# A block's weighted row sum in four column groups, and a bias product in two row groups and two banks: one change to a two-layer attention and expert kernel

## The chip, the cores and the metric

The kernel runs on one core of a Trainium2 chip. The time is device microseconds (us) of one execution; of the kernel before, three runs were timed, and a further one was profiled. The engines are TensorE (PE in the profile; its weight loads are PEld), VectorE (DVE), ScalarE (ACT), GpSimd (POOL) and SyncE (SP, which issues most DMAs).

## What is computed

Four sequences of 512 rows of 256 numbers go through two layers; each layer is an attention with a context of 1024 rows, and a mixture of experts of which each row takes two.

```python
# layer 0's attention (encoder_hc: the normed x; decoder_hq: the context)
Sim = (encoder_hc @ w1)[:, :, None] + (decoder_hq @ w2)[:, None, :] + jnp.einsum('bid,bjd->bij', encoder_hc * w3, decoder_hq) + b_sim[0]
A = jax.nn.softmax(Sim, axis=2)
hq_hat = jnp.einsum('bij,bjd->bid', A, decoder_hq)
Batt = jax.nn.softmax(jnp.max(Sim, axis=2), axis=1)
hc_bar = jnp.einsum('bi,bid->bd', Batt, encoder_hc)[:, None, :]        # the weighted row sum
feats = jnp.concatenate([encoder_hc, hq_hat, encoder_hc * hq_hat, encoder_hc * hc_hat], axis=-1)
hcq = feats @ W_qv + b_qv
...
# layer 1's experts: comb is a row's weight for each of 8 experts (two are not zero)
for e in range(8):
    a = jax.nn.gelu(_layernorm(xf, ln_w[e], ln_b[e]) @ fc1_w[e] + fc1_b[e], approximate=True)
    out = out + (a @ fc2_w[e] + fc2_b[e]) * comb[:, e:e + 1]           # fc2_b: the experts' biases
```

Two places of this are changed: `hc_bar`, the sum of a block's 512 rows with one weight each, and the sum over experts of `fc2_b[e] * comb[:, e]`, which the kernel makes for all rows by itself, as a product of `comb` and `fc2_b`.

## The kernel before

All data are 32-bit floats. A batch is 512 rows, four tiles of 128. The program is written with a tile framework whose scheduler orders each engine's instructions; TensorE's order is as written for the whole program, SP's for the experts' stages.

**Stages.** Layer 0's attention (`layer0_attention`, about 10 to 215 us) goes through the four batches: scores against the context (L315), softmax, transposes of the probabilities (L274), the attended context (L345), and the products with `W_qv` (L381). Work of neighbouring batches is interleaved by hand: `sim_finish` is a generator that is advanced piece by piece, between another batch's scores and transposes, and the routing of the batch before is a third strand. Then come layer 0's experts (to about 365), layer 1's attention (`layer1_attention`, to about 640) and layer 1's experts (the rest).

**The row sum** (`sim_finish`). With `mx` the rows' maxima, `gb` minus the block's maximum (one number copied to 128 partitions by L354), ACT makes `eb = exp(mx + gb)`, 128 partitions by four tiles, and its sum `es` (L359). L364 sums `es` over the partitions, L366 multiplies each tile's column of `eb` with the tile's 128x256 rows and accumulates the four in one row of PSUM, L370 and L372 divide on VectorE, and L393 turns the row of 256 into two columns of 128, which scale a part of `W_qv` (`weff`, L399). The order on TensorE about it: scores of the next batch (L315; in the last batch the routing's product L888), L364, L366, products L381.

**Layer 1's attention** runs 32 units (batch, tile, pair of heads). TensorE's order in one step: scores of a unit (L616, two groups of 64 array rows), first half of an older unit's transposes (a2t, L639, two banks of four), the output product of an older one (L679), its values (L664, two groups of 64 array columns) and a transpose (L670), a piece of the routing and the bias product, a piece of the next queries, and the second half of the a2t transposes. VectorE makes the scores' minimum with the mask (L625), ACT the exponential (L629), both copy the transposes from PSUM (L642, L644).

**The bias product** (`route_steps` with layer 1). `comb` (L980) is 128 x 4 tiles x 8 experts. L984 transposes the four tiles into 8 partitions x 512, L986 copies that on ACT, and L994 multiplies: for each pair of tiles two products of 8x128 with `fc2b` (8x256) into the two halves of one bank; L998 adds a pair to `x` on VectorE. The pairs of a batch are one step apart, except in the last batch. After the last one come the stores of `x` (L1000) and, for the last batch, the remaining scatters of rows (L951), two behind each entry of `L.biased`; layer 1's experts read those rows.

**PSUM.** Three pools of two buffers each: `ps_s` for scores, `ps_t` (`tr_ps`, transposes and small things) and `ps_m` (`mm_ps`, products). A tile of a pool waits for the release of the one before the last of that pool.

**Other lines that matter.** Gates' logits L888 use four groups of 32 array columns:

```python
nc.tensor.matmul(
    lt_ps[t * GROUP : t * GROUP + GROUP, :], gates[:, c, :], xT[:, c, bass.ts(t, P)],
    start=(c == 0), stop=(c == NC - 1),
)
```

GpSimd clears constants at the start, then issues the fills of the row buffers (L200, L207), which wait for the last first load, and adds `bqv` to `x` (L295). `wsim_row` (L305, for the last time at 173.5 us) and `bqv` (L295, 132.8 us) are single constants of 128x256.

Of the kernel before, what the change touches and what calls it, by code (L numbers as in the profile page):

```python
# [8 lines left out]
F32 = mybir.dt.float32  # L9
# [3 lines left out]
AF = mybir.ActivationFunctionType  # L13
ALU = mybir.AluOpType
# [3 lines left out]
P = 128  # L18
NB = 4
S = 512  # L20
NT = S // P
M = 1024
NJ = M // P
D = 256
# [3 lines left out]
EX = 8  # L28
# [8 lines left out]
GROUP = 32  # L37
# [26 lines left out]
def two_layers(ctx: ExitStack, tc: tile.TileContext, io, out):  # L64
    nc = tc.nc

    const = ctx.enter_context(tc.tile_pool(name="const", bufs=1))
# [4 lines left out]
    sm = ctx.enter_context(tc.tile_pool(name="sm", bufs=4))  # L72
# [9 lines left out]
    def t4(shape, name, dt=F32):  # L82
        return k4.tile(shape, dt, tag="k4", name=name)
# [4 lines left out]
    def tsmall(shape, tag, dt=F32):  # L88
        return sm.tile(shape, dt, tag=tag, name=tag, bufs=2 if tag[:3] in ("rt_", "tp_", "tt_") else None)
# [4 lines left out]
    def tr_ps(name):  # L94
        return ps_t.tile([P, 512], F32, tag="t", name=name)

    def mm_ps(name):
        return ps_m.tile([P, 512], F32, tag="m", name=name)


    ident = const.tile([P, P], F32, tag="ident", name="ident")
    make_identity(nc, ident)
    ones = const.tile([P, P], F32, tag="ones", name="ones")
# [40 lines left out]
    def small(name, shape, src, queue=nc.sync):  # L144
        t = const.tile(shape, F32, tag=name, name=name)
        queue.dma_start(out=t, in_=src)
        return t
# [5 lines left out]
    x = []  # L153
# [21 lines left out]
    bqv = small("bqv", [P, D], io["b_qv"].partition_broadcast(P), nc.gpsimd)  # L175
    wsim_row = small("wsim_row", [P, D], io["w_sim_row"].partition_broadcast(P), nc.gpsimd)
# [13 lines left out]
        nc.sync.dma_start(out=gates[:, :, at : at + n], in_=src.rearrange("(c p) e -> p c e", p=P))  # L190
    gate_b = small("gate_b", [P, ET0], io["expert_bias"].partition_broadcast(P))
    alpha = small("alpha", [P, EX], io["alpha"].partition_broadcast(P))
    fc2b = small("fc2b", [EX, D], io["fc2_b"])
    wq = small("wq", [P, NC, D], io["Wq"].rearrange("(c p) n -> p c n", p=P))
    wkv = small("wkv", [P, NC, 2 * D], io["Wkv"].rearrange("(c p) n -> p c n", p=P))
    wo = small("wo", [P, NC, D], io["Wo"].rearrange("(c p) n -> p c n", p=P))
# [2 lines left out]
    for e in range(EX):  # L199
        i = nc.gpsimd.dma_start(  # L200
            out=rows[e * REGION : (e + 1) * REGION, :].rearrange("(p k) r -> p k r", p=P),
            in_=zeros.unsqueeze(1).to_broadcast([P, REGION // P, ROW]),
# [5 lines left out]
        out=ys[:, :].rearrange("(p k) d -> p k d", p=P),  # L208
        in_=zeros[:, 0:D].unsqueeze(1).to_broadcast([P, 2 * NB * S // P, D]),
# [100 lines left out]
    def sim_scores(st, t):  # L310
# [12 lines left out]
        softmax_exp(p, spf, 1.0, nm)  # L323
        return p

    def sim_finish(st):

        b, xn, eT, aT = st["b"], st["xn"], st["eT"], st["aT"]

        mx = tsmall([P, NT], "b0_mx")  # L330
        nc.vector.scalar_tensor_tensor(mx, st["r"], bsim, st["negmax"], ALU.add, ALU.subtract)
        m1 = tsmall([P, 1], "b0_m1")
        nc.vector.tensor_reduce(m1, mx, AX.X, ALU.max)
        gp = tr_ps(f"g0_{b}")
        nc.tensor.transpose(gp[0:1, 0:P], m1, ident)
        g = tsmall([1, 1], "b0_g")
        nc.vector.tensor_reduce(g, gp[0:1, 0:P], AX.X, ALU.max, negate=True)

        hq = t4([P, NC, S], f"hqT_{b}")
        eh = t4([P, NC, S], f"ehT_{b}")  # L340

        def attend(c):
            op = mm_ps(f"hq_{b}_{c}")
            for j in range(NJ):
                nc.tensor.matmul(  # L345
                    op, ctxn[b][:, j, bass.ts(c, P)], aT[:, j, :], start=(j == 0), stop=(j == NJ - 1)
                )
            nc.scalar.copy(hq[:, c, :], op)
            st["attended"] = nc.vector.tensor_tensor(eh[:, c, :], op, eT[:, c, :], ALU.mult)

        attend(0)
        yield
        bp = tr_ps(f"gb0_{b}")
        nc.tensor.matmul(bp[:, 0:1], ones[0:1, :], g, start=True, stop=True)  # L354
        gb = tsmall([P, 1], "b0_gb")
        nc.vector.tensor_copy(gb, bp[:, 0:1])
        eb = tsmall([P, NT], "b0_eb")
        es = tsmall([P, 1], "b0_es")
        nc.scalar.activation(eb, mx, AF.Exp, bias=gb, accum_out=es)  # L359
        attend(1)  # L360
        yield

        hp = tr_ps(f"hc0_{b}")
        nc.tensor.matmul(hp[0:1, D : D + 1], es, ones[:, 0:1], start=True, stop=True)  # L364
        for t in range(NT):
            nc.tensor.matmul(  # L366
                hp[0:1, 0:D], eb[:, t : t + 1], xn[:, t, :], start=(t == 0), stop=(t == NT - 1)
            )
        rt = tsmall([1, 1], "b0_rt")
        nc.vector.reciprocal(rt, hp[0:1, D : D + 1])  # L370
        hr = sm.tile([1, D], F32, tag="b0_hr", name=f"b0_hr_{b}", bufs=1)
        nc.vector.tensor_scalar(hr, hp[0:1, 0:D], rt, None, ALU.mult)  # L372
        ops = {}

        def products(t, k, last):
            if not last:
                ops[t] = mm_ps(f"hcq_{b}_{t}")[:, 0:D]
            op = ops[t]
            for c in range(NC):
                for i, (l, w) in enumerate(k):  # L380
                    nc.tensor.matmul(  # L381
                        op, l[:, c, bass.ts(t, P)], w(c), start=(not last and c == 0 and i == 0),
                        stop=(last and c == NC - 1),
                    )

        late = [(hq, lambda c: wqv[:, 2 + c, :]), (eh, lambda c: wqv[:, 4 + c, :])]
        for t in range(2):
            products(t, late, False)
        yield

        hp = tr_ps(f"hcc0_{b}")
        for c in range(NC):
            nc.tensor.matmul(hp[:, c : c + 1], hr[:, bass.ts(c, P)], ones[0:1, 0:1], start=True, stop=True)  # L393
        hc = tsmall([P, NC], "b0_hc")
        nc.vector.tensor_copy(hc, hp[:, 0:NC])

        weff = sm.tile([P, NC, D], F32, tag="weff", name=f"weff_{b}", bufs=1)
        for c in range(NC):
            nc.vector.scalar_tensor_tensor(  # L399
                weff[:, c, :], wqv[:, 6 + c, :], hc[:, c : c + 1], wqv[:, c, :], ALU.mult, ALU.add  # L400
            )
        yield
        for t in range(NT):
            if t >= 2:
                products(t, late, False)
            products(t, [(eT, lambda c: weff[:, c, :])], True)
            nc.vector.tensor_tensor(x[b][:, t, :], ops[t], x[b][:, t, :], ALU.add)
            if t > 0:
                yield
# [122 lines left out]
    def mha_bias(st, t):  # L532

        if t == 0:
            st["mbias"] = t8([P, NT, M], f"mbias_{st['b']}", BF16)
        return nc.vector.tensor_scalar(
            st["mbias"][:, t, :], st["mask"][:, t, :], 1.0, MASKED, ALU.subtract, ALU.mult
        )
# [143 lines left out]
    def layer1_attention(sts):  # L682
# [3 lines left out]
        units = []  # L686
        for b in range(NB):
            units += [(b, t, n) for t in range(NT) for n in range(NC)]
        ps, aTs = {}, {}
        routes, queries = {}, None  # L690
        kvs = mha_kvs(sts, (NB - 1,))
        done = None
        for i in range(len(units) + 4):
            if i < len(units):
                b, t, n = units[i]
                ps[i] = mha_scores(sts[b], n, t)
                unit = sts[b]
                if i + 1 < len(units) and units[i + 1][0] > 0 and units[i + 1][2] == 0:
                    bias = mha_bias(sts[units[i + 1][0]], units[i + 1][1])
# [4 lines left out]
            if 0 <= i - 2 < len(units):  # L704
                b, t, n = units[i - 2]
# [5 lines left out]
            if 0 <= i - 4 < len(units):  # L711
                b, t, n = units[i - 4]
                if n == NC - 1:
                    added = mha_out(sts[b], t)
            if 0 <= i - 3 < len(units):
                b, t, n = units[i - 3]
# [11 lines left out]
            b = i // (2 * NT) + 1  # L728
# [9 lines left out]
            b, k = divmod(i - 11, 2 * NT)  # L738
# [76 lines left out]
    L1 = Layer(1, EX, FF1 // P, ET0, None)  # L815
# [57 lines left out]
    def route_steps(L, b):  # L873
# [12 lines left out]
        for c in range(NC):  # L886
            for t in range(NT):
# [3 lines that stand above are left out]
# [13 lines left out]
        buf, xn = st["buf"], st["xn"]  # L904
        shape = [P, 2, NT, ne]
        pick = tsmall(shape, "rt_pick")
# [17 lines left out]
        at = tsmall([P, NT, ne], "rt_atp")  # L924
# [45 lines left out]
        if L.n == 0:  # L970
            for t in range(NT):
                xs = x[b][:, t, :]
# [3 lines left out]
            return  # L976

        nc.vector.tensor_tensor(pick, pick, wk.unsqueeze(3).to_broadcast(shape), ALU.mult)
        comb = tsmall([P, NT, EX], "rt_comb")
        nc.vector.tensor_tensor(comb, pick[:, 0], pick[:, 1], ALU.add)  # L980
        yield
        cp = tr_ps(f"cT_{b}")
        for k in range(NT):
            nc.tensor.transpose(cp[0:EX, bass.ts(k, P)], comb[:, k, :], ident)  # L984
        cT = t4([EX, S], f"combT_{b}")
        nc.scalar.copy(cT, cp[0:EX, :])  # L986
        yield
        L.biased = []
        for k in range(0, NT, 2):
            if k > 0 and b + 1 < NB:  # L990
                yield
            op = mm_ps(f"b2_{b}_{k}")
            for j in range(2):
                nc.tensor.matmul(  # L994
                    op[:, bass.ts(j, D)], cT[:, bass.ts(k + j, P)], fc2b, start=True, stop=True
                )
            xs = x[b][:, k : k + 2, :]
            L.biased.append(nc.vector.tensor_tensor(xs, op.rearrange("p (j d) -> p j d", d=D), xs, ALU.add))  # L998
        written.append(
            nc.sync.dma_start(out=flat[b * S : (b + 1) * S, :].rearrange("(t p) d -> p t d", p=P), in_=x[b])  # L1000
        )
# [476 lines left out]
```

## Time and profile before

| what | us |
|---|---|
| timed runs | 918.59 (median), 915.99, 918.94 |
| the profiled execution | 917.38 |
| its span, first to last instruction | 915.60 |
| PE busy, 47 to 200 us (153.0) | 148.7 |
| PE busy, 400 to 520 us (120.0) | 117.0 |
| PE busy, 520 to 600 us (80.0) | 75.8 |
| VectorE busy, 520 to 600 us | 57.0 |
| ScalarE busy, 520 to 600 us | 49.8 |
| PE busy, 640 to 690 us (50.0) | 46.5 |
| PE busy, 690 to 916 us (225.6) | 215.8 |

How to read the lines below. A group's line has: line, engine and operation, what it writes <- what it reads, shapes (for a matmul, array rows * columns in use, then the shape), count | busy us, mean ns of one | idle before it, and what ended the idle time. A timeline's line has start, length in us, engine, line, operation, count, and in brackets the idle time before it with its releaser. Neighbouring records of one group are merged, and a matmul's length reaches to its modelled end, so that of two lines of PE the starts say more than the lengths. A product of 32-bit floats is two matmul records, a transpose one. All times are of the one profiled execution, counted from its first instruction.

### The profile page before, as it was taken

Reading aid. Unit: us, or ns where it says so; the run is one execution under the profiler, and the core shown is the slowest. Engines: PE = TensorE matmul, PEld = TensorE weight load, DVE = VectorE, ACT = ScalarE, POOL = GpSimd, SP = SyncE. Lnnn points to the kernel's source line nnn. Section 1 sums busy time; section 2 is a strip of 40 time slices with the busy share of each in tenths; the row PEclk is TensorE's granted clock in tenths of the full one; section 3 lists DMA queues with packets and bytes.
Section 4 is the critical chain, followed back from the end, with each engine's and each line's share of the span. In section 5 each row is a group of like instructions: output and inputs, shape, how many; then the busy total and the mean of one; then the engine's idle time right before and its main releaser. Section 6 shows DMA issues by size and latency. Waiting matters only on the chain.

```text
span 915.6 us, 15375 instructions
## 1 busy us (share of the span) xinstructions
PE 868.2 (95%) x5578; PEld 659.9 (72%) x5578; DVE 426.1 (47%) x1253; ACT 334.2 (36%) x749; POOL 226.2 (25%) x276
## 2 busy tenths in 40 slices
PE   6899999998999998999999999999989999999995
PEld 2456464755699996556676666667879999999995
DVE  5646473736623331765675686676721111111120
ACT  4323331222211111475574565565512333222231
POOL 2303014044313222000130250351642122122122
PEclk9999999999999999999999999999999999999999
DMA  8999933030188893600000123221257956877961
GB/s 309 293 261 245 246 134 112 15 101 35 54 276 262 252 347 116 229 24 1 24 2 1 46 69 119 71 70 56 74 158 247 304 168 193 262 238 239 322 213 22
DMA packets 55028, 142.08 MB, mean 155 GB/s; under 512 B 6894, under 2 KB 32933, under 8 KB 48800
## 3 DMA queue, kind: packets, MB, share of 16 engines
q1 hardware_dynamic: 39264, 102.89, 33.5%
q0 software_dynamic: 15392, 38.10, 16.4%
q8 instruction: 48, 0.79, 0.3%
q14 instruction: 36, 0.29, 0.1%
q10 hardware_dynamic: 288, 0.00, 0.0%
HBM read 131.52 MB, written 39.91 MB: 187 GB/s over the span
## 4 chain that ended last, share of the span: by engine, by line
PE 43%; DVE 7%; issue 4%; ACT 4%; DMA 2%; POOL 0%; SPq 0%; POOLq 0%; ACTq 0%; DVEq 0%
PE hp L1145 12%; PE y L1170 11%; PE s L616 5%; PE a2t L639 4%; PE o L664 4%; ACT p L629 2%; DVE p L625 2%; PE q L600 1%; ACT a2T L644 1%; PE hp_ahead L1145 1%; PE ht L1120 1%; PE wo L679 1%; DMA ys<-yw,to 1%; PE o L670 1%; DMA yb<-ys 1%
## 5 line engine op out<-in xcount | busy, mean ns | idle before, releaser
L1154 ACT ACTIVATE aT<-hp,w1s 128x128 f32<-128x128 f32 x248 | 67.3, 382 | 163.3 <-issue 153.2
L1145 PEld LDWEIGHTS hp<-hT,w1s 128*128 128x128 f32 x992 | 115.8, 192 | 2.4 <-DVE hT L1126 0.8
L1145 PE MATMUL hp<-hT,w1s 128*128 128x128 f32 x992 | 116.1, 275 | 0.6 <-DVE hT L1126 0.6
L1170 PE MATMUL y<-w2s,aT 128*128 128x256 f32 x496 | 112.3, 379 | 0.5 <-ACT aT L1154 0.5
L1170 PEld LDWEIGHTS y<-w2s,aT 128*128 128x128 f32 x496 | 91.8, 190 | 11.9 <-ACT aT L1154 0.7
L629 ACT ACTIVATE p<-p,s_nm 128x1024 f32<-128x1024 f32 x64 | 73.5, 1148 | 73.3 <-DVE s_nm L625 73.2
L625 DVE CUSTOM_DVE_ANT_0 p<-s,mbias 128x1024 f32<-128x1024 f32 x64 | 75.7, 1221 | 38.7 <-PE s L616 38.6
L1188 POOL DMA_INDIRECT out<-yw,to x31 | 47.8, 1541 | 168.1 <-DMA out<-yw,to 59.6
L1174 DVE TENSOR_SCALAR yw<-y,row 128x256 f32<-128x256 f32 x59 | 28.6, 484 | 122.3 <-PE y L1170 122.3
L951 POOL DMA_INDIRECT rows<-rowbuf,rt_posi x64 | 64.2, 1004 | 81.8 <-DVE rt_posi L931 25.4
L639 PEld LDWEIGHTS a2t<-ident,p 128*128 128x128 f32 x512 | 56.2, 142 | 36.8 <-issue 21.7
L639 PE MATMUL a2t<-ident,p 128*128 128x128 f32 x512 | 70.8, 278 | 5.7 <-DVE xn2T L594 2.6
L616 PE MATMUL s<-kT,q2T 64*128 64x512 f32 x256 | 65.1, 615 | 0.7 <-DVE s_nm L625 0.7
L664 PE MATMUL o<-a2T,v 128*64 128x128 f32 x1024 | 63.3, 276 | 0.1
L315 PE MATMUL s<-ctxT,q0T 128*128 128x512 f32 x128 | 62.4, 634 | 0.7 <-ACT q0T L292 0.7
L664 PEld LDWEIGHTS o<-a2T,v 128*64 128x64 f32 x1024 | 55.4, 137 | 8.5 <-issue 6.8
L644 ACT COPY a2T<-a2t 128x512 f32<-128x512 f32 x96 | 53.3, 582 | 16.1 <-PE a2t L639 16.1
L1126 DVE TENSOR_SCALAR hT<-ht,w1s 128x128 f32<-128x128 f32 x62 | 22.6, 406 | 77.3 <-PE ht L1120 71.2
L345 PE MATMUL hq<-a0T,ctxn 128*128 128x512 f32 x128 | 56.8, 596 | 0.1
L1145 PEld LDWEIGHTS hp<-hT,w0s 128*128 128x128 f32 x448 | 54.3, 192 | 3.2 <-DVE hT L1122 1.8
L1145 PE MATMUL hp<-hT,w0s 128*128 128x128 f32 x448 | 55.0, 276 | 1.0 <-DVE hT L1122 1.0
L1170 PE MATMUL y<-w0s,aT 128*128 128x256 f32 x224 | 53.1, 380 | 0.7 <-ACT aT L1150 0.7
(258 smaller groups left out, 1206.8 us busy)
## 6 DMA issues: line engine op xcount, KB each, us to landing
w1s<-in_w1p SPq DMA_DIRECT2D x34, 1030.0 KB
w2s<-in_w2p SPq DMA_DIRECT2D x34, 1024.0 KB
rows<-zeros POOLq DMA_DIRECT2D x8, 2064.0 KB
w0s<-in_w1p SPq DMA_DIRECT2D x31, 512.0 KB
w0s<-in_w2p SPq DMA_DIRECT2D x31, 512.0 KB
row<-rows SPq DMA_DIRECT2D x59, 129.0 KB
ctxT<-in_ctxT SPq DMA_DIRECT2D x4, 1024.0 KB
ctxn<-in_ctx SPq DMA_DIRECT2D x4, 1024.0 KB
```

Source lines behind the costliest of these rows:

```text
L315: nc.tensor.matmul(sp[:, h, :], st["qT"][:, c, bass.ts(t, P)], ctxT[b][:, c, bass.ts(h, 512)], start=(c == 0), stop=(c == NC - 1),)
L345: nc.tensor.matmul(op, ctxn[b][:, j, bass.ts(c, P)], aT[:, j, :], start=(j == 0), stop=(j == NJ - 1))
L616: nc.tensor.matmul(sps[r][:, k, :], st["qT"][at, n, bass.ts(t, P)], st["kT"][at, n, bass.ts(k, 512)], start=True, stop=True,)
L625: nc.vector.tensor_tensor_reduce(p, sps[r].rearrange("p h n -> p (h n)"), st["mbias"][:, t, :], -ATT_SCALE, -ATT_SCALE * LEAST, ALU.add, A ...
L629: nc.scalar.activation(p, p, AF.Exp, bias=nm, scale=-1.0, accum_out=tot[:, r : r + 1])
L639: nc.tensor.transpose(pt[:, bass.ts(j, P)], p[:, bass.ts(4 * g + j, P)], ident)
L644: nc.scalar.copy(d, pt)
L664: nc.tensor.matmul(op[r * HD : r * HD + HD, :], st["v"][:, j, bass.ts(2 * n + r, HD)], aT[:, r, bass.ts(j, P)], start=(j == 0), stop=(j == ...
L951: i = nc.gpsimd.indirect_dma_start(out=rows[:, :], out_offset=bass.IndirectOffsetOnAxis(ap=pos_i[:, k, t : t + 1], axis=0), in_=buf[:, k, ...
L1145: nc.tensor.matmul(o, w1[:, c * ff + f * P : c * ff + f * P + P], hT[:, c, :], start=(c == 0), stop=(c == NC - 1),)
L1154: nc.scalar.activation(aT[:, f, :], hp[:, f // 4, bass.ts(f % 4, P)], AF.Gelu_apprx_tanh, bias=w1[:, at : at + 1])
L1170: nc.tensor.matmul(op, aT[:, f, :], w2[:, f * D : f * D + D], start=(f == 0), stop=(f == nf - 1))
```

## The change

The row sum: each tile's weights `eb` become a column of a cleared 128x32 block, and the four products go to four groups of 32 array columns (32 output partitions each), not accumulated over each other; the denominator is made on all 128 partitions with a matrix of ones; L393's product, now over 128 partitions, adds the four groups, of which only the first row of each isn't zero. The bias product: `comb` has 32 columns for each tile (8 in use, the rest cleared once), so one 128x128 transpose takes all four tiles, tile t in partitions 32t to 32t+7; `fc2b` is loaded four times to these partitions; the two products of a pair use two groups of array rows, and go to two banks, one of `ps_m` and one of `ps_t`; each tile is added by itself. `fc2b` and `comb` take the places of `wsim_row` and `bqv`; `fc2b` is loaded in layer 1's attention instead of at the start.

```diff
@@ -190,7 +190,6 @@
-    fc2b = small("fc2b", [EX, D], io["fc2_b"])
@@ -323,6 +322,10 @@
+    eb = const.tile([P, NT, GROUP], F32, tag="eb", name="eb")
+    nc.gpsimd.memset(eb, 0.0)
@@ -354,22 +357,21 @@
-        eb = tsmall([P, NT], "b0_eb")
         es = tsmall([P, 1], "b0_es")
-        nc.scalar.activation(eb, mx, AF.Exp, bias=gb, accum_out=es)
+        nc.scalar.activation(eb[:, :, 0], mx, AF.Exp, bias=gb, accum_out=es)
...
-        nc.tensor.matmul(hp[0:1, D : D + 1], es, ones[:, 0:1], start=True, stop=True)
+        nc.tensor.matmul(hp[:, D : D + 1], ones, es, start=True, stop=True)
         for t in range(NT):
             nc.tensor.matmul(
-                hp[0:1, 0:D], eb[:, t : t + 1], xn[:, t, :], start=(t == 0), stop=(t == NT - 1)
+                hp[t * GROUP : t * GROUP + GROUP, 0:D], eb[:, t, :], xn[:, t, :], start=True, stop=True
             )
-        rt = tsmall([1, 1], "b0_rt")
-        nc.vector.reciprocal(rt, hp[0:1, D : D + 1])
-        hr = sm.tile([1, D], F32, tag="b0_hr", name=f"b0_hr_{b}", bufs=1)
-        nc.vector.tensor_scalar(hr, hp[0:1, 0:D], rt, None, ALU.mult)
+        rt = tsmall([P, 1], "b0_rt")
+        nc.vector.reciprocal(rt, hp[:, D : D + 1])
+        hr = sm.tile([P, D], F32, tag="b0_hr", name=f"b0_hr_{b}", bufs=1)
+        nc.vector.tensor_scalar(hr, hp[:, 0:D], rt, None, ALU.mult)
@@ -390,7 +392,7 @@
-            nc.tensor.matmul(hp[:, c : c + 1], hr[:, bass.ts(c, P)], ones[0:1, 0:1], start=True, stop=True)
+            nc.tensor.matmul(hp[:, c : c + 1], hr[:, bass.ts(c, P)], ones[:, 0:1], start=True, stop=True)
@@ -686,6 +688,12 @@
+        L1.fc2b = const.tile([P, D], F32, tag="wsim_row", name="fc2b")
+        for t in range(NT):
+            nc.sync.dma_start(out=L1.fc2b[t * GROUP : t * GROUP + EX, :], in_=io["fc2_b"])
+        L1.comb = const.tile([P, NT, GROUP], F32, tag="bqv", name="comb")
+        nc.gpsimd.memset(L1.comb, 0.0)
@@ -976,26 +984,24 @@
-        comb = tsmall([P, NT, EX], "rt_comb")
-        nc.vector.tensor_tensor(comb, pick[:, 0], pick[:, 1], ALU.add)
-        yield
-        cp = tr_ps(f"cT_{b}")
-        for k in range(NT):
-            nc.tensor.transpose(cp[0:EX, bass.ts(k, P)], comb[:, k, :], ident)
-        cT = t4([EX, S], f"combT_{b}")
-        nc.scalar.copy(cT, cp[0:EX, :])
+        nc.vector.tensor_tensor(L.comb[:, :, 0:EX], pick[:, 0], pick[:, 1], ALU.add)
+        yield
+        cp = tr_ps(f"cT_{b}")[:, 0:P]
+        nc.tensor.transpose(cp, L.comb.rearrange("p t e -> p (t e)"), ident)
+        cT = t4([P, P], f"combT_{b}")
+        nc.scalar.copy(cT, cp)
         yield
         L.biased = []
         for k in range(0, NT, 2):
             if k > 0 and b + 1 < NB:
                 yield
-            op = mm_ps(f"b2_{b}_{k}")
-            for j in range(2):
-                nc.tensor.matmul(
-                    op[:, bass.ts(j, D)], cT[:, bass.ts(k + j, P)], fc2b, start=True, stop=True
-                )
-            xs = x[b][:, k : k + 2, :]
-            L.biased.append(nc.vector.tensor_tensor(xs, op.rearrange("p (j d) -> p j d", d=D), xs, ALU.add))
+
+            for t, op in ((k, mm_ps(f"b2_{b}_{k}")), (k + 1, tr_ps(f"b2_{b}_{k + 1}"))):
+                at = slice(t * GROUP, t * GROUP + EX)
+                nc.tensor.matmul(op[:, 0:D], cT[at, :], L.fc2b[at, :], start=True, stop=True)
+                xs = x[b][:, t, :]
+                added = nc.vector.tensor_tensor(xs, op[:, 0:D], xs, ALU.add)
+            L.biased.append(added)
```

## The prediction

> **What bounds the kernel now.** I read the page's engine totals and chain first, then busy time by stretches, the groups by form, and last the timeline around each edited place.
>
> ```profile
> PE 868.2 (95%) x5578; PEld 659.9 (72%) x5578; DVE 426.1 (47%) x1253; ACT 334.2 (36%) x749; POOL 226.2 (25%) x276
> ...
> PE 43%; DVE 7%; issue 4%; ACT 4%; DMA 2%; POOL 0%; SPq 0%; POOLq 0%; ACTq 0%; DVEq 0%
> ```
>
> TensorE (PE) is busy for 95% of the span and leads the chain. By stretches, PE is busy 50.8 of 53 us from 47 to 100, 49.3 of 50 to 150 and 48.6 of 50 to 200: layer 0's attention, where the row sum lies, is PE's own queue. From 520 to 600 it is busy 75.8 of 80 with VectorE (DVE) at 57.0 and ScalarE (ACT) at 49.8: there the chain passes from one to another. From 690 on PE runs weights against tiles.
>
> ```profile
> L994 PE MATMUL b<-fc2b,combT 8*128 8x256 f32 x32 | 9.0, 400 | 0.2 <-DVE yw_ahead L1174 0.2
> ...
> L366 PE MATMUL hc<-xn,b_eb 128*1 128x256 f32 x32 | 7.5, 378 | 0.0
> ...
> L888 PE MATMUL lgT<-xn0rT,gates 128*32 128x128 f32 x64 | 2.6, 279 | 0.0
> ...
> L984 PE MATMUL cT<-ident,rt_comb 128*8 128x128 f32 x16 | 2.4, 273 | 0.2 <-ACT a2T L644 0.2
> ```
>
> An f32 product shows as two passes, so 32 records of the row sum L366 are 4 batches of 4 tiles. They take 7.5 us busy, 0.23 a pass of 256 columns. L888 already does what the change wants: four groups of 32 array columns, 64 passes of 128 columns in 2.6 us, 0.041 a pass.
>
> **Row sum in four groups of columns.** Before, batch 0:
>
> ```profile
> 57.96 1.45 PE L315 MATMUL s<-ctxT,q0T 128*128 128x512 f32 x3
> ...
> 59.34 0.19 PE L364 MATMUL hc<-ones,b_es 128*1 128x1 f32 x2
> ...
> 59.40 1.89 PE L366 MATMUL hc<-xn,b_eb 128*1 128x256 f32 x8
> ...
> 61.21 0.70 PE L381 MATMUL hcq<-wqv,hqT 128*128 128x256 f32 x2
> ```
>
> The eight passes start 0.215 apart. The scores before them end at 59.25 (last start 58.82 and 0.43 a pass), the array stands still for 0.09, and after the last pass ends at 61.12 again 0.09. From 59.25 to 61.21 this place costs 1.96 us, and nothing else of PE lies beside it.
>
> ```profile
> 105.16 0.64 PE L888 MATMUL lgT<-xn0rT,gates 128*32 128x128 f32 x16
> ...
> 105.73 0.70 PE L315 MATMUL s<-ctxT,q0T 128*128 128x512 f32 x1
> ```
>
> In L888 single records start in fours, 0.007 apart, each four 0.11 to 0.13 after the four before: passes of different column groups run together. So eight passes of 256 columns are two fours: 0.24 to the second four, 0.02 for its own stagger, 0.215 for the last pass: 0.475. Ahead of them the denominator now loads 128x128 ones (two passes of one column, 0.11 to 0.13 each: L393, which also loads 128 columns, steps by that), where the 128x1 sum took 0.05. Then 0.17 to change to column groups (L393's last pass to the next load is 0.17). Sum: 0.11+0.17+0.475+0.09 = 0.85 instead of 1.96: 1.11 less for each of batches 0 to 2.
>
> [...] The trace shows the stop (0.09 each way), but 128x1 already pays it on both sides, so nothing is added for batches 0 to 2. In batch 3 the logits' groups L888 stand directly before the sum; ones 128x128 between them puts in one more: 0.1 to 0.2.
>
> Batch 3 has another limit. Its products L381 start at 201.92; 1.0 us sooner they would wait for VectorE's ehT, done at 201.19, which frees their bank. I take 201.25, a gain of 0.67.
>
> The column L393 gets weights of 128 rows instead of one. It still steps by 0.11. With one row the scores after it start 0.17 late and lose another 0.1 on an uncovered weight load (second pass 0.53 after the first, 0.43 in the run); with 128 rows there is no change of mode. I take 0.17 for three batches, bounds 0 and 0.25.
>
> Reciprocal and scaling widen from one partition to 128 at the same free size: 0.155 and 0.471 now, and 128x256 forms stand at 0.41 to 0.48. Nothing. `eb` written with a stride of 32 in place of 1: 128x4 either way, 0.3. The memset of `eb` on GpSimd is one of 512 bytes; `done`, which is written much later in the program and also waits for nothing, is cleared at 4.9 us, while `eb` is first written at 49.1. Were it queued behind the fills (last issue at 68.4), batch 0 would lose about 9 us (59.3 to 68.5); the early memsets speak against it, and I leave 2% to it.
>
> Layer 0: 3 x 1.11 + 3 x 0.17 + 0.67 = 4.5 us, bounds 3.0 and 4.9. What follows (routing, tiles, the rows read back) is a chain behind this work, and its weights come early (issued at 154 and 199.7, used at 251), so it moves forward whole.
>
> **One transpose for four.** Four passes at 0.109 become one, 0.33 less of PE. In batches 0 and 1 something else is last:
>
> ```profile
> 522.83 0.57 ACT L986 COPY combT<-cT 8x512 f32<-8x512 f32 x1
> ...
> 523.45 0.66 PE L639 MATMUL a2t<-ident,p 128*128 128x128 f32 x4 [0.72 <-ACT combT L986]
> ```
>
> ACT's copy frees the bank that the next transposes want. Its cost goes by the free size: 128x128 (L672, s_rT) takes 0.25, so 0.57 becomes 0.25 and PE starts 0.32 sooner; PE's own 0.33 turns into waiting. Batch 2 (638.65) runs in PE's queue: 0.33. Batch 3 (658.2) lies beside VectorE's table: nothing. Together 1.0, bounds 0.5 and 1.1. ScalarE gains 1.3 us, mostly idle time.
>
> **Products in two groups of rows and two banks.** A pair's four passes step 0.32, 0.22, 0.22, 0.22. Two groups of rows make it 0.32 and 0.22, like the two groups of 64 rows in L616, which start in twos 0.007 apart: 0.43 less a pair. Two such groups at once with 8 rows are not in the trace; the modes' stops are (0.09 after L994), so K=8 pays them already. From below: nothing gained if the two don't run together.
>
> But the second bank is one of the two that the transposes use. After it comes a2t's first half in the other bank, then its second half, which must now wait until VectorE has added. Before, nothing of PE stood behind that addition. What VectorE does there:
>
> ```profile
> 603.18 1.09 PE L639 MATMUL a2t<-ident,p 128*128 128x128 f32 x8
> ...
> 603.55 0.17 DVE L631 RECIPROCAL s_tot<-s_tot 128x2 f32<-128x2 f32 x1 [1.30 <-ACT p L629]
> 603.64 0.29 DVE L673 TENSOR_TENSOR oT<-o,s_rT 128x128 f32<-128x128 f32 x1
> 603.84 0.68 DVE L536 TENSOR_SCALAR mbias<-mask 128x1024 bf16<-128x1024 uint8 x1
> ...
> 604.44 0.68 DVE L998 TENSOR_TENSOR x<-b,x 128x512 f32<-128x512 f32 x1
> ```
>
> One addition of 128x512 (0.69) becomes two of 128x256 (0.415 each, L680), 0.75 with their overlap. If the order stays, both end at 605.20, and the half that started at 603.66 starts at 605.25: 1.6 late, with the next scores and VectorE's p (606.22) behind it. At 537.2 the order is the same (additions end at 540.5, the half was at 538.7); 1.9 late, of which about 1.1 reach the end, as p was held to 542.0 by other work. In the other two pairs (530.0, 594.9) the addition is VectorE's next work but one: product out at 595.64, additions until 596.43, the half at 596.47 against 596.49 before. The 0.43 is spent on the wait: 0. [...]
>
> For 537.2 and 602.1 the order is the scheduler's: additions at once cost nothing, the old order 2.7. The trace has both orders at neighbouring places; I take half, 1.3. The last two pairs (664.2, 665.5) lie beside VectorE's chain to the last scatters; the first addition's end moves from 666.43 to 666.50: 0.1 later.
>
> So +0.5 - 1.3 - 0.1 = -0.9; bounds +1.7 (also 0.3 at each of the four) and -2.4.
>
> **Loads.** fc2b's one issue at 22.0 (0.38 of SP) goes; four come, into a place free since 173.9. SP's queue issues two loads at 199.7 and 200.1 and then nothing until 242.5. Issued amid the tile table's loads they would hold a row load by 1.5 us; PE then has keys and values to multiply until 250.7. I take 0, bounds 0 and -1. The clearing of `comb` comes after 135, far ahead of 515.
>
> **Sum.** 4.5 + 1.0 - 0.9 - 0 = 4.6. The profiled execution took 917.38 (915.60 span and 1.8 around it): 912.8. The median of the runs shown, 918.59, is 1.2 above it; I forecast against that: 914.0. A difference of 0.3% (2.8 us) is about what a measurement of this kernel can tell.
>
> **Rivals.**
> 1. *VectorE's order is good everywhere*: the stalls go, 4.5+1.0+0.5: 6.0, up to 7.2. 912.0. The trace's pairs at 530 and 594.9 speak for it.
> 2. *Gain given back*: the row sum saves 4.5, but both stalls come whole (2.7), two transposes don't pay (0.5 left), and a load costs 1: about 1.5 to 2. 917.0. For it speaks that the order at 602 was chosen with the same instructions.
> 3. *Slower*: the additions fall behind oT and mbias at all four pairs of the attention, so that a2t's second half waits 1.65, 1.9, 1.55 and 1.6 us, 6.7 in all, with the next scores behind it. That outruns 4.5+1.0+0.5 = 6.0 and, with the two pairs of additions and a late load, gives 919.5 to 922. It decides when the stalls sum to over 6.0, that is 1.5 at each pair. Against it: two of the four have the addition ahead of oT today.
> 4. *The groups don't run together* (the sum of 256 columns in series): only transposes and the column gain, 1.0+0.5-2.4: 919. L888 speaks against it.
>
> **Chances.** Forecast (912.8 to 915.5) 48%; rival 1 20%; rival 2 18%; rival 3 and a late `eb` 10%; rival 4 4%. Faster by over 0.3%: nearly all of the first two, 0.66; within 0.3%: 0.25; slower by over 0.3%: 0.09. Range 911.0 to 918.5.
>
> **What would show it.** L366 with 32 columns, starts in fours, about 0.26 us between first and last start; from scores to L381 0.85. A later batch's row sum earlier by 1.3 each. combT at 0.25. In the pairs a2t's second half with a wait on L998's successor: under 0.2 at 530 and 595, up to 1.9 at 537 and 602. The forecast is wrong if the time before 400 us isn't 4 to 5 us shorter, or if PE waits for VectorE's additions more than 3 us in all.

## The result, and the profile after

| | before | after |
|---|---|---|
| median of 20 runs each, us | 917.68 | 914.29 |
| lowest and highest | 915.82 to 919.77 | 909.30 to 919.75 |
| the profiled execution | 917.38 | 914.49 |
| its span | 915.60 | 912.7 |

The ratio is 0.997, with an interval of 0.996 to 0.998: 3.4 us less by the medians. Beside other runs of before, 12 more of the changed kernel gave 914.77 and 0.9948 (0.9926 to 0.997). The prediction had 914.0 in a range of 911.0 to 918.5.

The page's engine totals and its chain by engine, after:

```profile
PE 862.9 (95%) x5566; PEld 658.2 (72%) x5566; DVE 427.4 (47%) x1261; ACT 333.8 (37%) x749; POOL 226.2 (25%) x278
...
PE 43%; DVE 7%; ACT 5%; issue 4%; DMA 1%; POOL 0%; SPq 0%; ACTq 0%; POOLq 0%; DVEq 0%
```

TensorE (PE) lost 5.3 us of busy time and the span 2.9. The groups by form of the edited products:

```profile
L1001 PE MATMUL b<-fc2b,combT 8*128 8x256 f32 x32 | 6.3, 426 | 0.9 <-DVE yw_ahead L1180 0.9
...
L368 PE MATMUL hc<-xn,eb 128*32 128x256 f32 x32 | 2.6, 391 | 0.0
L366 PE MATMUL hc<-b_es,ones 128*128 128x1 f32 x8 | 1.2, 222 | 0.0
```

The row sum (L368) went from 7.5 to 2.6 us busy and the bias product (L1001) from 9.0 to 6.3. A pass is not shorter (391 ns against 378): several run at once. The denominator (L366) now has a row of 1.2. The two products alone lost 7.6; the trace of after also has three stretches with TensorE's clock at half rate, against one in before's (last section), and there the same work is busy for longer (in the one at 663.6 us the passes of L1151 start 0.213 apart, ahead of it 0.112). The timeline about the row sum of batch 0, after:

```profile
56.32 1.88 PE L314 MATMUL s<-ctxT,q0T 128*128 128x512 f32 x4
58.04 0.28 PE L366 MATMUL hc<-b_es,ones 128*128 128x1 f32 x2
58.25 0.64 PE L368 MATMUL hc<-xn,eb 128*32 128x256 f32 x8
58.82 0.70 PE L383 MATMUL hcq<-wqv,hqT 128*128 128x256 f32 x2
```

The last scores start at 57.61 and end at 58.04; the products L383 start at 58.82. The place costs 0.78, where it cost 1.96. The passes start in fours 0.007 apart, at 58.25 and 58.49.

**By places.** The start of one and the same PE instruction in each trace, minus its start in before's trace, tells where time was won or lost. The columns are traces; the last four are experiments of the next section. Down to the last scores ahead of batch 0's row sum, TensorE's instructions are the same in all of them, so what stands there already does not come from the change.

| start of | after | after again | one group | late fill | late fill, one bank | late fill, sums first |
|---|---|---|---|---|---|---|
| batch 1's first scores (34.6) | -0.67 | -0.31 | +0.08 | +0.16 | -0.60 | -0.61 |
| last scores ahead of batch 0's row sum (58.8) | -1.21 | -0.77 | -0.06 | +0.20 | -1.22 | -1.22 |
| batch 0's hcq, L383 (61.2) | -2.40 | -1.96 | +0.03 | -0.98 | -2.40 | -2.41 |
| batch 1's hq (85.3) | -0.44 | +0.71 | +1.91 | -1.06 | -2.48 | -2.49 |
| batch 1's hcq (111.2) | -0.66 | +0.18 | +2.01 | -2.25 | -3.67 | -3.68 |
| batch 2's hq (135.5) | -0.74 | +0.10 | +2.00 | -2.33 | -3.75 | -3.76 |
| batch 2's hcq (160.2) | -1.93 | -1.09 | +2.09 | -3.52 | -4.93 | -4.95 |
| batch 3's hq (183.6) | -2.01 | -1.17 | +2.10 | -3.60 | -5.02 | -5.03 |
| batch 3's hcq (201.9) | -2.89 | -2.05 | +2.49 | -4.48 | -5.89 | -5.91 |
| layer 1's scores, unit 18 (516.3) | -4.24 | -2.69 | +2.84 | -5.32 | -6.71 | -6.63 |
| first ahead expert product (641.3) | -3.74 | -0.51 | +4.99 | -4.84 | -7.45 | -7.60 |
| end (915.6) | -2.90 | -0.21 | +6.00 | -4.25 | -5.19 | -5.58 |

The early differences come with the clock. In before the first scores start 0.85 us apart up to 16.86 us and 0.43 apart from there, and the trace's first record of the granted clock, at 1.00, starts at 16.83; in after that record starts at 15.06 and the step changes at 15.07, which is worth half of the 1.8 between them. The rest comes at the half-rate stretch, which lies at 33.9 in before and at 32.1 in after.

From the last scores to batch 0's hcq lies the first row sum: -1.18 or -1.19 wherever four groups run. From a later batch's hq to its hcq lies another: -1.19 in batch 2 and -0.88 in batch 3. In batch 1 it is -0.22 and -0.53 in the two traces of after, which have a half-rate stretch of the clock at 83 us (the last section), and -1.19 in the late-fill ones, which have none. Two things in the columns of after were not forecast: 1.96 and 2.67 us are lost between batch 0's hcq and batch 1's hq, and layer 1's attention loses 0.5 between unit 18 and the first expert product (2.2 in the second trace, which has a half-rate stretch there, at 602.7). The experiments take these up, and the row sum itself.

### The profile page after: what moved, and what is told of

Same layout as the page of the kernel before. It is cut to its first block, busy times and chain, and to the rows that moved or that the text cites. A ratio compares the mean times of both kernels' runs of the same rounds, so it can differ in the third digit from the quotient of the medians.

```text
span 912.7 us, 15370 instructions
## 1 busy us (share of the span) xinstructions
PE 862.9 (95%) x5566; PEld 658.2 (72%) x5566; DVE 427.4 (47%) x1261; ACT 333.8 (37%) x749; POOL 226.2 (25%) x278
## 4 chain that ended last, share of the span: by engine, by line
PE 43%; DVE 7%; ACT 5%; issue 4%; DMA 1%; POOL 0%; SPq 0%; ACTq 0%; POOLq 0%; DVEq 0%
PE hp L1151 12%; PE y L1176 11%; PE s L618 5%; PE a2t L641 4%; PE o L666 4%; ACT p L631 3%; DVE p L627 2%; PE hp_ahead L1151 1%; PE q L602 1%; ACT a2T L646 1%; PE ht L1126 1%; PE wo L681 1%; PE v L512 1%; DMA ys<-yw,to 1%; DMA yb<-ys 1%
## 5 line engine op out<-in xcount | busy, mean ns | idle before, releaser
L1151 PEld LDWEIGHTS hp<-hT,w1s 128*128 128x128 f32 x992 | 115.8, 192 | 2.4 <-DVE hT L1132 0.8
L1151 PE MATMUL hp<-hT,w1s 128*128 128x128 f32 x992 | 116.1, 275 | 0.6 <-DVE hT L1132 0.6
L1151 PEld LDWEIGHTS hp<-hT,w0s 128*128 128x128 f32 x448 | 54.4, 192 | 2.9 <-DVE hT L1128 1.5
L1151 PE MATMUL hp<-hT,w0s 128*128 128x128 f32 x448 | 54.9, 275 | 1.0 <-DVE hT L1128 1.0
```

The costliest lines, as they stand in the source:

```text
L1151: nc.tensor.matmul(o, w1[:, c * ff + f * P : c * ff + f * P + P], hT[:, c, :], start=(c == 0), stop=(c == NC - 1),)
```

## The experiments

Theory A, the prediction's: the gain is the row sum's passes running four at a time; the pairs in two banks cost time where VectorE's additions stand behind other work. Rival B: the gain comes from elsewhere (the bias product, or leaving the mode of one column, 128*1 in the records). Ratios are to runs of before on the same chip: one chip for the first four experiments, another for the next four kernels, a third for the last two.

**The row sum alone.** Before, with the row sum's part of the diff and `fc2b` loaded once, late; the bias product as in before.

> The kernel before with the row sum's part of the change alone (and fc2b loaded once, late, into wsim_row's place). Theory: the four column groups save 1.1 to 1.3 us of TensorE's own queue in each of four batches, and what follows moves forward whole: 3.5 to 4.5 us less than before, that is about 913.5, or all of the gain of the whole change. Rival: the gain is lost on the way (a later wait takes it), and the bias product is what saved time: 0 to 1.5 less than before, 916.5.

Measured: 913.3 against 919.05, ratio 0.9942 (0.9925 to 0.9958), so 3.9 to 6.9 us less. Batch 2's hq to hcq is 1.18 shorter, batch 3's 0.88. From unit 18 to the first expert product the difference to before is constant to 0.01 us: what was won earlier passes through whole.

**The bias product alone.** The change with the row sum, the denominator and L393 as in before.

> The changed kernel with the row sum as it was before: the bias product's part alone. Theory: 0.3 us saved by the shorter copy in batches 0 and 1 and by the transposes in batch 2, 0.5 by the pairs of batch 2, and about 2.3 lost where a second half of the a2t transposes waits for VectorE's additions (two places): within 1 us of before, about 917.5, and in the trace two waits of a2t of 1.0 to 1.3 us. Rival: the two row groups gain at every pair: 3 us less than before, 914.7.

Measured: 920.42 against the same 919.05, 1.001 (0.9996 to 1.0025): it gains nothing. Its steps from unit 18 on are nearly those of after: -0.28 at batch 0's transpose, +0.98 and then -0.68 at its second pair, -0.30 at batch 1's transpose, +0.98 at its second pair (+1.27 in after), -0.56 in batch 2. The medians of the two halves, -5.75 and +1.37, add up to -4.4; the whole change gave -3.4 and -4.05.

**The bias product of batches 0 and 1 as before.**

```diff
+        if b < 2:
+            cp = tr_ps(f"cT_{b}")
+            for k in range(NT):
+                nc.tensor.transpose(cp[0:EX, bass.ts(k, P)], L.comb[:, k, 0:EX], ident)
...
```

> The changed kernel with the bias product of batches 0 and 1 as before (four transposes, a pair into one bank, one addition). Theory: the two waits for the additions go (2.3 us), the shorter copy goes too (0.6): 1.2 to 2 us less than the changed kernel, about 912.7. Rival, that those waits were not on the path that sets the end: 0 to 1 us more than the changed kernel, 914.8.

Measured: 915.1, 0.9939 (0.9913 to 0.9964). The gain in batch 2 stays (-0.55), and the loss of the second pairs is gone with their gains: unit 18 to the first expert product -0.54 instead of +0.50 in after. The median lies nearer to the rival's 914.8 than to 912.7, and its interval holds both: only the stretch in the trace tells.

**One transpose, one bank.** The pair's products one after the other in one bank of `ps_m`, each over 64 rows of `combT` with `fc2b` between zeros, and one addition of 512 columns.

```diff
-            for t, op in ((k, mm_ps(f"b2_{b}_{k}")), (k + 1, tr_ps(f"b2_{b}_{k + 1}"))):
+            op = mm_ps(f"b2_{b}_{k}")
+            at = slice(k * GROUP, (k + 2) * GROUP)
+            for j in range(2):
+                nc.tensor.matmul(op[:, bass.ts(j, D)], cT[at, :], L.fc2b[j][at, :], start=True, stop=True)
```

> The changed kernel with a pair's two products in one bank of ps_m again and one addition of 128x512 (64 rows of combT, fc2b in two constants that are zero but for the even or the odd tiles), with one transpose for four kept. Theory: no a2t waits for an addition, and each pair takes 0.43 us more of TensorE: two waits of 1.0 to 1.3 gone, 0.5 lost in batch 2: 1.5 to 2 us less than the changed kernel, about 912.5, and 5 less than before. Rival: the pairs' two banks were worth their 0.43 at each of the places: 1 to 2 us more than the changed kernel, 916.

Measured: 912.07, 0.993 (0.9906 to 0.9954). The second pair of batch 1, first in after, then here:

```profile
597.68 1.17 PE L1001 MATMUL b<-fc2b,combT 8*128 8x256 f32 x4
...
598.78 0.66 PE L641 MATMUL a2t<-ident,p 128*128 128x128 f32 x4
...
599.35 0.17 DVE L633 RECIPROCAL s_tot<-s_tot 128x2 f32<-128x2 f32 x1 [1.58 <-ACT p L631]
599.43 0.29 DVE L675 TENSOR_TENSOR oT<-o,s_rT 128x128 f32<-128x128 f32 x1
...
599.64 0.74 DVE L1003 TENSOR_TENSOR x<-b,x 128x256 f32<-128x256 f32 x2
...
600.44 0.66 PE L641 MATMUL a2t<-ident,p 128*128 128x128 f32 x4 [1.00 <-DVE x L1003]
```

```profile
598.28 1.13 PE L1006 MATMUL b<-fc2b,combT 64*128 64x256 f32 x4
...
599.34 1.09 PE L641 MATMUL a2t<-ident,p 128*128 128x128 f32 x8
...
599.99 0.17 DVE L633 RECIPROCAL s_tot<-s_tot 128x2 f32<-128x2 f32 x1 [1.58 <-ACT p L631]
...
600.36 1.13 PE L618 MATMUL s<-kT,q2T 64*128 64x512 f32 x4
...
600.88 0.68 DVE L1008 TENSOR_TENSOR x<-b,x 128x512 f32<-128x512 f32 x1
```

In after the eight transposes stop half-way for 1.00 us, until VectorE has added; the additions stand behind s_tot and oT, which wait for ScalarE's exponential. With one bank all eight transposes run through, and the addition may come after the next scores have begun. From unit 18 to the first expert product this gains 0.72 (-0.28, -0.30, -0.13 at the three transposes, and nothing at the pairs).

**All four tiles in one group.**

```diff
-                hp[t * GROUP : t * GROUP + GROUP, 0:D], eb[:, t, :], xn[:, t, :], start=True, stop=True
+                hp[0:GROUP, 0:D], eb[:, t, :], xn[:, t, :], start=(t == 0), stop=(t == NT - 1)
...
```

The scaling and L393 read only the 32 rows that are written.

> The changed kernel with all four tiles' weight columns in ONE group of 32 array columns, accumulated over each other as before; the blocks of 32 columns, the denominator on 128 partitions and everything else stay. Theory A (the row sum's gain is that four groups run together): eight passes 0.215 apart again, so row sum longer by 1.2 in each of batches 1 and 2, and by 0.9 in batch 3, nothing in batch 0 (its gain is lost at a fixed place later): 3.3 us slower than after, about 917.6. Theory B (the gain comes from leaving the mode of one column, or from the wider column product behind it): no more than 0.5 slower, 914.8.

Measured, beside the changed kernel once more:

> The changed kernel once more, beside the three others on the same chip. Expected 913.5 to 915.5, 0.995 to 0.997 of before; junk (batch 1's first row product) again stretched to 3 to 4 us by GpSimd's fill and sum at 69 to 73 us.

921.53 against 914.77 and, of before, 918.82; ratios 1.0028 (1.0007 to 1.0049) and 0.9948. Batch 2 with one group, and its group's row:

```profile
158.56 1.88 PE L314 MATMUL s<-ctxT,q0T 128*128 128x512 f32 x4
160.27 0.28 PE L366 MATMUL hc<-b_es,ones 128*128 128x1 f32 x2
160.48 1.91 PE L368 MATMUL hc<-xn,eb 128*32 128x256 f32 x8
162.32 0.70 PE L383 MATMUL hcq<-wqv,hqT 128*128 128x256 f32 x2
```

```profile
L368 PE MATMUL hc<-xn,eb 128*32 128x256 f32 x32 | 7.7, 382 | 0.0
```

The same blocks, the same denominator, the same number of instructions, and the eight passes take 1.84 us again. From hq to hcq batches 1 and 2 are 0.10 and 0.08 slower than before, batch 3 0.40. So the row sum's gain is that the groups run together; without that, the change makes it a loss, and from the denominator's first pass to the sum's it is 0.21 us now where it was 0.05.

The forecast of +3.3 over after was too small (6.8 by the medians). The row sums of batches 1 to 3 are 3.8 of it (1.28, 1.27 and 1.28 more than with four groups; batch 1 against the late-fill trace, as after has a half-rate stretch there). Batch 0's is another 1.27, which the forecast had put at nothing; with it the four are 5.1. The rest is not settled.

**The late fill.** What is lost between batch 0's hcq and batch 1's hq? GpSimd (POOL) and VectorE (DVE) in after's timeline, then in before's:

```profile
68.69 1.64 POOL L206 DMA_DIRECT2D ys<-zeros  x1 [20.14 <-issue]
69.08 0.41 DVE L409 TENSOR_TENSOR x<-hcq,x 128x256 f32<-128x256 f32 x1
...
69.42 3.58 DVE L304 CUSTOM_DVE_ANT_0 junk<-xn,wsim_row 128x256 f32<-128x256 f32 x1
...
70.28 2.42 POOL L294 TENSOR_TENSOR x<-x,bqv 128x1024 f32<-128x1024 f32 x1
...
72.92 0.41 DVE L409 TENSOR_TENSOR x<-hcq,x 128x256 f32<-128x256 f32 x1
```

```profile
68.37 1.64 POOL L207 DMA_DIRECT2D ys<-zeros  x1 [19.72 <-issue]
...
71.90 0.80 DVE L305 CUSTOM_DVE_ANT_0 junk<-xn,wsim_row 128x256 f32<-128x256 f32 x1
```

One row product `junk` takes 3.58 us (0.42 on average in batches 2 and 3). It begins while GpSimd issues the fill of the results' buffer and ends 0.3 after GpSimd's sum of x and bqv. In before the fill came at 68.37, but VectorE reached `junk` only at 71.90, and it took 0.80. In after `junk` began 0.73 us into the issue of the fill (68.69 to 70.33) and 0.86 ahead of that sum (70.28 to 72.70). That the issue held it first and the sum behind it is an estimate from these times; this trace does not show the two apart. The experiment puts the fill behind the last batch's sum:

```diff
-    ys_fill = nc.gpsimd.dma_start(
...
+        if b == NB - 1:
+            ys_fill.append(
+                nc.gpsimd.dma_start(
...
```

> The changed kernel with one more edit: GpSimd issues the fill of the row buffer of results behind the sum of x and bqv of the LAST batch (132 us) instead of ahead of the second batch's. Theory A (batch 0's gain was lost because VectorE stands still while GpSimd issues that fill at 68.7 and does the second batch's sum behind it): that sum runs at about 48 us, junk at 69.4 takes 0.41 instead of 3.58, the stretch from hcq of batch 0 to hq of batch 1 is 24.0 to 24.5 instead of 25.99, and the time 1.5 to 2 us less than after: 912.5. Theory B (the stretch is set by something else, or the sum at 48 us stops VectorE just as long there): no change, 914.3.

Measured:

```profile
49.55 1.12 POOL L199 DMA_DIRECT2D rows<-zeros  x1 [11.55 <-DMA ctxn<-in_ctx]
...
50.62 2.44 POOL L290 TENSOR_TENSOR x<-x,bqv 128x1024 f32<-128x1024 f32 x1
...
70.83 0.41 DVE L308 CUSTOM_DVE_ANT_0 junk<-xn,wsim_row 128x256 f32<-128x256 f32 x1
```

The sum runs at 50.6 and `junk` takes 0.41. From batch 0's hcq to batch 1's hq it is 23.95 us instead of 25.99 (24.04 in before), and 23.95 in the three other traces with a late fill: theory A's stretch. The time is 913.85 (0.9941, 0.9917 to 0.9964) against after's 914.77 in the same comparison; the intervals overlap, so of the 1.5 to 2 us expected only the stretch in the trace is shown. The fill has moved its stop to 133 us, where TensorE doesn't wait for it:

```profile
133.59 0.24 DVE L939 TENSOR_TENSOR rt_tmp<-rt_pick,rt_atp 128x96 f32<-128x96 f32 x1
...
133.84 1.09 DVE L932 COPY run<-run 128x12 f32<-128x12 f32 x1
133.90 1.04 DVE L941 TENSOR_REDUCE rt_pos<-rt_tmp 128x8 f32<-128x96 f32 x1
134.06 1.01 DVE L868 TENSOR_SCALAR rowbuf<-x,ln_mv,ln_rs 128x256 f32<-128x256 f32 x1
```

The fill's issue (133.26 to 134.94) alone holds a copy of 12 numbers per partition for 1.09 us; three such copies take 0.15 on average in before.

That the early fill costs this time is shown, but not that the row sum's gain brings it about. In the eight traces with the early fill it comes at 68.4 to 71.8 us; what it waits for, behind eight other fills, the profile does not say. The kernel with one group, which gains nothing in batch 0, meets it just as well:

```profile
71.29 1.65 POOL L206 DMA_DIRECT2D ys<-zeros  x1 [22.48 <-issue]
71.93 3.67 DVE L304 CUSTOM_DVE_ANT_0 junk<-xn,wsim_row 128x256 f32<-128x256 f32 x1
```

It loses 1.88 there, and the bias product alone, with the old row sum, 2.84. The stretch is 24.75 to 26.9 us in seven of the eight traces (25.9 to 26.0 in one group and one bank, which have no half-rate stretch in it; the two of after have part of one); the one trace of before has the earliest fill and 24.04. How often other executions of before lose time there no run shows, and before with a late fill was not run.

**Late fill and one bank together.**

> Both edits together: the pair's two bias products one after the other in one bank with one addition of 512 columns (64 rows, fc2b between zeros), and the late fill. Expected from the two parts: 1.3 less by the pairs and 1.5 to 2 less by the fill, 914.3 - 3 = 911, 0.991 to 0.993 of before. If the fill only moves the stop, 913.

Measured: 912.25, 0.9928 (0.9903 to 0.9954). Once more, in the comparison of the next kernel:

> The kernel of e8_fill_onebank once more, beside e9_addfirst on the same chip. Expected 911 to 913, 0.990 to 0.994 of before, and the same differences by place as in its first trace, half-rate windows of TensorE's clock apart.

912.89, 0.9944 (0.9923 to 0.9965). In the first trace the -2.40 at batch 0's hcq is -2.48 at batch 1's hq, and layer 1's attention gains 0.74.

**Two banks, the sums first.** Two groups of rows and two banks stay; in a step with a pair VectorE's additions must go ahead of s_tot and oT (on the kernel with the late fill).

```diff
+            if L1.added is not None and i < len(units):
+                for late in (unit["unit"], scaled):
+                    after(late, L1.added, "the sums go before")
```

> The kernel of e7_fill (the change with the late fill) with one more dependency: in a step of layer 1's attention that has a pair of bias products, VectorE's two additions to x go ahead of s_tot and oT of that step; two groups of rows and two banks stay. Theory A (the pairs in two banks lose because the additions stand behind s_tot and oT, which wait for ScalarE's exponential, and the second half of the a2t transposes waits for the additions to free its bank): the wait of 1.0 ahead of that half at the second pairs goes, and layer 1's attention from unit 18 to the first expert product gives a gain of 0.7 (as with one bank) to 1.2 instead of the loss of 0.5 in after and e7_fill; the time is 1.3 less than e7_fill, about 912.5, the same as e8_fill_onebank. Theory B (the loss comes with the two groups of rows or the second bank itself, whatever VectorE's order): it still loses 0.5 there, 913.9.

Measured: 911.7, 0.995 (0.9932 to 0.9967), with before at 916.87. The second pair of batch 1:

```profile
595.04 0.98 PE L1009 MATMUL b<-fc2b,combT 8*128 8x256 f32 x4
...
595.77 0.76 DVE L1011 TENSOR_TENSOR x<-b,x 128x256 f32<-128x256 f32 x2 [0.83 <-PE b L1009]
595.95 1.28 PE L645 MATMUL a2t<-ident,p 128*128 128x128 f32 x8
...
596.65 0.17 DVE L637 RECIPROCAL s_tot<-s_tot 128x2 f32<-128x2 f32 x1
```

The eight transposes run nearly through, and unit 18 to the first expert product gains 0.97 where the same kernel without the dependency loses 0.48 and after 0.50. TensorE's waits for the additions, in us, times and longest, in after and here:

```profile
PE a2t L641 <- DVE x L1003: 2.5, 4, 1.0
```

```profile
PE a2t L645 <- DVE x L1011: 0.8, 3, 0.3
```

So it is VectorE's order, not the second bank or the two groups, that costs: theory A. The times don't show this gain: the ratio is 0.995 here and 0.9941 with the late fill alone, from two comparisons whose intervals overlap. Nor can they choose between the last two versions; both beat before, and in the stretches above both gain over after.

## Why the prediction was right, point by point

**The row sum.** Forecast: 1.11 a batch, 0.17 behind L393, 0.67 in batch 3, 4.5 in all. Measured at the places: 1.18 (batches 0 to 2) and 0.88; behind L393 0.07 to 0.08 in batches 0 to 2, and 0.19 in batch 3. That is 4.8 within bounds of 3.0 to 4.9. The stop of 0.09 between scores and sum, which I had counted, is not there: L366 follows the scores' end at once. Batch 3's limit took 0.3 of 1.18, not 0.44.

**"It moves forward whole."** This was not so behind batch 0. I had followed what comes after layer 0, not what stands on VectorE between batch 0's row sum and batch 1: `junk`, which ran into GpSimd's fill. Against before's trace that costs 1.96, more than the row sum gains there. A row for this was in the trace of before, a `p` (L267) of 3.74 us at 32.84 beside GpSimd's first fills, while the other 15 of its group average 0.75. But as kernels without the gain lose time there too, the 1.96 is not simply the gain given back. The row sum's 4.8 would be worth 2.9 if before always escapes the fill, and all of 4.8 if before meets it as after does. That the row sum alone is 3.9 to 6.9 faster speaks for the upper part.

**One transpose.** Forecast 1.0: 0.32, 0.32 and 0.33. Measured 0.29 and 0.30 in batches 0 and 1, by the reason given: ScalarE's copy begins as late as before and takes 0.27 instead of 0.57:

```profile
518.60 0.27 ACT L992 COPY combT<-cT 128x128 f32<-128x128 f32 x1
...
518.92 0.66 PE L641 MATMUL a2t<-ident,p 128*128 128x128 f32 x4 [0.70 <-ACT combT L992]
```

In batch 2 it was 0.13 to 0.14 (the one-bank kernels, where the pairs are neutral). Batch 3's, put at nothing, is 0.27. In all 1.0 as forecast, which is luck: two sizes were off, in opposite directions.

**The pairs.** Forecast a loss of 0.9: gains 0.5, stalls 1.3, tables 0.1. Measured: +0.29 at batch 0's second pair (0.97 late, of which 0.68 was caught up, as forecast for that place), +1.27 at batch 1's, 0.05 at each first pair, -0.43 in batch 2, +0.06 at the next. No run shows the 0.5 as a term; in its place stand this 0.43 gained and 0.06 lost. At the last two pairs TensorE gains 0.15 instead of losing 0.1. Loss 1.1, up to there. Ten us further on TensorE waits for a load of rows (2.58 us in before, 1.77 in after), so how much of the last pairs' gain reaches the end is open. The stalls were neither of my two orders: the additions went ahead of mbias, but stayed behind s_tot and oT. TensorE's waits for them come to 2.5 us, under the 3 that I had set as a mark.

**The sum.** The row sum's 4.8, the transposes' 1.0 and the pairs' loss of 1.1 make 4.7, and 2.7 if the whole loss at the fill counts. The medians show 3.4 and 4.05, between the two; the forecast was 4.6. That 914.0 came within 0.3 us is in part luck: it was taken from a median of three runs, 918.59, and against the 917.68 of twenty it would have been 913.1. Of the rivals, the given-back gain (2) has a counterpart in one place that it did not name; the slower end (3) had its mechanism right at two pairs out of four, with a wait of 1.00 at each (0.26 at the others); the groups that do not run together (4) are refuted by the one-group kernel.

**The trace alone would have misled.** The forecast named a sign of being wrong: not 4 to 5 us earlier before 400 us. In after TensorE stands at -4.23 there, which looks right. But 1.21 of it was there before its first changed instruction (+0.20 to -3.27 over all traces), so that the change had given only 3.0. Of these, 0.94 lie about a copy of the logits before the values v: VectorE starts it 0.07 after its input in the first trace of after, 1.5 after it in the second trace of the same kernel, and 2.3 after it in before, with nothing else on VectorE and GpSimd issuing row scatters beside it; the cause is open. The second trace is only at -2.68, 1.9 without its early part. So by its own sign the step "moves forward whole" failed for the kernel as it was changed; with the late fill it is 5.0 to 5.5 without the early part. The first two columns of the table, one kernel, differ by 2.7 at the end.

## What to carry to other kernels

Short products with few output rows can share the array: four groups of 32 columns made a serial run of 1.84 us one of 0.57, and the sign of it is that their records start together. Before booking a gain further down, follow each engine that lies between it and the next such place, above all one whose work is timed by something else, here a DMA issue on GpSimd that VectorE then ran into. Count differences between two traces from the last common instruction ahead of the change: up to 3.3 us stood there already. Whoever splits a result over two banks has to see what stands ahead of the emptying on its engine: the same products cost 0.5 us or gained 1.0, by VectorE's order alone.

## What the runs showed of the hardware

TensorE's granted clock fell to half for stretches of 3.413 us, in a kernel that keeps TensorE 95% busy: at 32 to 34 us in ten of the twelve traces (33.9 in before, 32.1 in after), and otherwise at times that differ from run to run (83.3 and 663.6 in after). Stretches of after: the 3.4 us ahead of its three, and one of these (columns: stretch, its length, busy us and instructions of PE, PEld, DVE, ACT and POOL, granted clock, DMA share, GB/s):

```profile
28.70:32.10 3.40, 1.15 (x9) 0.80 (x7) 3.01 (x7) 1.83 (x4) 3.05 (x3) 1.00 0.95 302
79.90:83.30 3.40, 1.71 (x12) 1.14 (x12) 3.24 (x8) 1.82 (x3) 1.05 (x1) 1.00 1.02 239
660.20:663.60 3.40, 2.52 (x19) 1.72 (x19) 3.40 (x14) 0.00 (x0) 2.01 (x3) 1.00 0.17 55
```

```profile
663.60:667.00 3.40, 3.40 (x19) 3.40 (x18) 0.03 (x1) 0.00 (x0) 2.79 (x3) 0.50 0.76 257
```

Each of them follows 3.4 us in which TensorE was busy 34% to 74%. But 48% did not always bring one; two further stretches of after, in a row:

```profile
670.40:673.80 3.40, 1.63 (x9) 1.18 (x8) 0.70 (x2) 0.00 (x0) 0.84 (x1) 1.00 0.80 148
673.80:677.20 3.40, 3.40 (x18) 3.01 (x18) 1.21 (x5) 0.00 (x0) 0.74 (x1) 1.00 0.40 48
```

So the busy share of the profile alone does not tell when the clock falls. The starts of after's three stretches lie 51.20 and 580.27 us apart, 15 and 170 times the 3.413; what sets the fall was not shown. The charge at 663.6 is 1.71 us (from 655 to 669 us of before's time after loses 1.27, where the kernel with the sums first, without such a stretch there, gains 0.44), half of 3.413. The traces have one to four such stretches ahead of 900 us (one in before, three in after), which goes with runs of one kernel lying up to 10 us apart: over after's 20 runs, time and mean granted clock correlate with -0.71.

With the late fill, the issue of one fill by GpSimd (133.26 to 134.94) held VectorE's operations at 133.84, 133.90 and 134.06 until it was over, even a copy of 12 numbers that began 0.58 us into it and took 1.09. It did not hold everything: the TENSOR_TENSOR at 133.59, which began 0.33 us into the same issue, took 0.24, as in before (0.235).
